# Routing logits and ranks of a mixture of experts: 32-column weights and moving tokens in place of 128-column weights, with a transpose behind

## Chip, cores and metric

The kernel runs on one core of one Trainium2 chip. The metric is the device time of an execution in microseconds. Three runs of the kernel before gave 1860.09, 1860.68 and 1863.35 us, median 1860.68.

## What is computed

The reference is a two-layer gated block over x, 16 batches of 256 tokens with 256 features. Each layer adds an attention part and a feed-forward part. Only the first feed-forward part, a router with 8 experts, is touched by the change:

```python
logits = x @ router_w.T                       # x: 4096 normed tokens x 256, router_w: 8 x 256
probs = softmax(logits, axis=-1)
topk_vals, topk_idx = top_k(probs, 2)
topk_w = topk_vals / (topk_vals.sum(-1, keepdims=True) + 1e-06)
expert_out = einsum('nh,eho->eno', x, expert_weights)
combined = take_along_axis(expert_out.transpose(1, 0, 2), topk_idx[:, :, None], axis=1)
out = ((combined.transpose(1, 0, 2) + remap_bias) * weights).sum(axis=0)
```

Around it stand a cross-attention with 16 heads ahead (333 keys a batch), a cross-attention over 77 context rows behind, and a chunked gated linear attention at the end. All is in float32.

## The kernel before

The program has four stages, one after the other, and a second, slow version of them (`fast` false) behind a branch that the profiled execution does not take.

The first stage, `stage0_fast` (L564), is the first attention. It works in units of a batch b and a group g of four heads, 64 units. The order on each engine is written out by hand: `dve`, `act`, `pool` and `pe` are `Pinned` (L42), which keeps every instruction in program order. A unit does, in this order: `scores(b, g)` (TensorE, then exponentials on ScalarE), `sums` on GpSimd, then `values` of the unit before (rows named o), and by g: `turn` and `project` at g = 1, `all_values(b + 1)` at g = 2, and always `heads` (rows named qk) of the unit ahead. `values` ends in two VectorE instructions, a reciprocal and a product (L742, L743). TensorE's o matmuls write four column tiles: head h goes to partitions 32h to 32h + 31 (L725, L739). `heads` leaves its keys to a VectorE copy (L690) and its queries to ScalarE (L689).

PSUM is handed out in pairs of banks, four of them in turn (L569 to L575): each new tile takes the pair used four tiles ago, once its reader is done.

The router's work for earlier batches is slipped between these steps by three tables (L761 to L767). `route.logits` of batch b - 1 stands behind `values` at g = 3 and `route.ranks` of batch b - 2 behind `values` at g = 2. Those of the last batches stand in the second stage, in its own table (L1201), beside the experts' matmuls.

- `logits` (L428): with the normed tokens turned to `xnT` (features on partitions), the tokens are the stationary operand, 128 tokens a time, and the router's 8 columns move. Four matmul calls a batch write tokens on partitions, 16 columns. ScalarE copies them to SBUF (`copied`, L436). `exps` and `choose` (L441, L450) find the two experts of every token.
- `ranks` (L507) counts, for each token and expert, the tokens ahead of it in the batch that go to the same expert: a triangle `before` and a square of ones are stationary, the choices `hs` move (16 columns each). ScalarE copies 32 columns. `place` (L514) turns the counts into rows.
- `scatter` writes each token's weighted copies to the experts' rows in DRAM by an indirect DMA from GpSimd.

`clear_rows` (L555) fills those rows with zeros ahead of it: 16 DMAs of 640 KB on SP's queue, from a tile of 128 x 256 zeros that is read repeatedly. It is called in the second unit (L810), and SP takes its instructions in order; the stores of the context's values (L662) and the load of them for batch 1 (L664) come behind it.

The second stage multiplies the experts' rows; the third and fourth are the second layer. In the fourth, a step in `stage3_fast` (L1858 to L1873) writes sums to four column tiles, with the rows `den`, and turns them back by a VectorE transpose, rows `dens`. It is in the kernel already and is not edited.

Of the kernel before, what the change touches and what calls it, by code (L numbers as in the profile page):

```python
# [10 lines left out]
F32 = mybir.dt.float32  # L11
I32 = mybir.dt.int32
AF = mybir.ActivationFunctionType
ALU = mybir.AluOpType
# [3 lines left out]
P = 128  # L18
B, S, D = 16, 256, 256
# [7 lines left out]
def bc(ap, shape, *axes):  # L27

    for a in axes:
        ap = ap.unsqueeze(a)  # L30
    return ap.to_broadcast(list(shape))
# [42 lines left out]
def layers(ctx: ExitStack, tc: tile.TileContext, t, out, check):  # L74
    nc = tc.nc
# [6 lines left out]
    def const(name, shape, dtype=F32):  # L82
        return cp.tile(list(shape), dtype, tag=name, name=name)
# [11 lines left out]
    def load_w(name, rows, cols, pool=cp):  # L95
        w = pool.tile([P, rows // P, cols], F32, tag=name, name=name)
        src = t[name].rearrange("(k p) f -> p k f", p=P)
        step = min(rows // P, max(1, (1 << 20) // (P * cols * 4)))
        for k in range(0, rows // P, step):
            nc.sync.dma_start(out=w[:, k:k + step, :], in_=src[:, k:k + step, :])  # L100
        return w
# [4 lines left out]
    ws1 = s1.enter_context(tc.tile_pool(name="s1w", bufs=1, side="right"))  # L106
# [34 lines left out]
    wo0 = load_w("wo0h" if fast else "wo0", 1024, D, w0)  # L141
    for b in range(2, B):
        load_x(b)
    rw1 = load_w("rw1", D, 8, ws1)
    ew1 = load_w("ew1", D, 2048, ws1)
    prio = const("prio", [P, 8])
    nc.sync.dma_start(out=prio, in_=t["prio"])
# [1 line left out]
    if fast:  # L149
        bv, own, pmask = (w12.tile(shape, F32, tag=n, name=n) for n, shape in (  # L150
            ("bv", [P, D]), ("own", [P, 2, 32]), ("pmask", [P, 2])))
        before, offs = (ws1.tile(shape, F32, tag=n, name=n) for n, shape in (
            ("before", [P, P]), ("offs", [P, 2, 2, 8])))

        gbo = const("gbo", [P, D])
        for n, x in (("bv", bv), ("bo", gbo), ("own", own), ("pmask", pmask), ("before", before),
                     ("offs", offs)):
            nc.sync.dma_start(out=x, in_=t[n])
    else:
        brow = w12.tile([1, 2, D], F32, tag="brow", name="brow")  # L160
        nc.sync.dma_start(out=brow, in_=t["brow"])
        bmask = w12.tile([P, 4], F32, tag="bmask", name="bmask")
        nc.sync.dma_start(out=bmask, in_=t["bmask"])
# [4 lines left out]
    ones = const("ones", [P, P])  # L168
# [6 lines left out]
    dve, act, pool, pe = (Pinned(tc, x) for x in (nc.vector, nc.scalar, nc.gpsimd, nc.tensor))  # L175
# [219 lines left out]
    class Route:  # L395
# [31 lines left out]

        def logits(self, b, bank):  # L428
            ps, xnT = bank("rt"), self.xnT.pop(b)
            for i in range(2):  # L430
                for k in range(2):
                    pe.matmul(ps[:, 8 * i:8 * i + 8], xnT[:, k, i * P:(i + 1) * P], rw1[:, k, :],
                              start=k == 0, stop=k == 1)
            self.copied(b, ps[:, :16])

        def copied(self, b, ps):  # L436
            n = ps.shape[1]
            self.ps[b] = ws1.tile([P, n], F32, tag=f"copied{n}", name="copied")
            act.copy(self.ps[b], ps)

        def exps(self, b):  # L441

            z = self.ps.pop(b)[:, :16].rearrange("p (i e) -> p i e", i=2)
            mx = st.tile([P, 2], F32, tag="rmx", name="rmx")
            dve.tensor_reduce(mx, z, AX.X, ALU.max)
            e = self.e[b] = st.tile([P, 2, 8], F32, tag="re", name="re")
            dve.tensor_tensor(e, z, bc(mx, [P, 2, 8], 2), ALU.subtract)
            act.activation(e, e, AF.Exp)
# [58 lines left out]
        def ranks(self, b, bank):  # L507
            hs, h1, h2 = self.hs[b]
            ps = bank("rank")
            pe.matmul(ps[:, :16], before, hs[:, 0].rearrange("p i e -> p (i e)"), start=True, stop=True)  # L510
            pe.matmul(ps[:, 16:32], ones, hs[:, 1].rearrange("p i e -> p (i e)"), start=True, stop=True)
            self.copied(b, ps[:, :32])

        def place(self, b):  # L514

            (_, h1, h2), ps, count = self.hs.pop(b), self.ps.pop(b), check["rows"][:, b // 8]
            base = st.tile([P, 2, 2, 8], F32, tag="base", name="base")
            at = st.tile([P, 2, 2, 2, 8], F32, tag="at", name="at")
            row = st.tile([P, 2, 2, 2], F32, tag="row", name="row")
            n = st.tile([P, 2, 8], F32, tag="nth", name="nth")  # L520
            dve.tensor_tensor(n, ps[:, :16].rearrange("p (i e) -> p i e", i=2), bc(count, [P, 2, 8], 1), ALU.add)
            dve.tensor_tensor(count, count, ps[:, 24:32], ALU.add)
            dve.tensor_tensor(n[:, 1, :], n[:, 1, :], ps[:, 16:24], ALU.add)
            dve.tensor_tensor(base[:, 0], n, offs[:, 0], ALU.add)

            dve.scalar_tensor_tensor(base[:, 1], n, ROWS - 1.0, offs[:, 1], ALU.min, ALU.add)
            for k, h in enumerate((h1, h2)):
                dve.tensor_tensor(at[:, :, :, k], base, bc(h, [P, 2, 2, 8], 1), ALU.mult)
            dve.tensor_reduce(row, at, AX.X, ALU.add)
            dve.tensor_copy(self.pos[:, b], row)  # L530
# [19 lines left out]
    def by_expert(rows, e):  # L550

        n = ALL_ROWS if rows in route.rows else ROWS
        return rows[e * n:e * n + ROWS].rearrange("(p n) d -> p n d", p=P)

    def clear_rows():  # L555
        zero = ws1.tile([P, D], F32, tag="zero", name="zero")
        nc.gpsimd.memset(zero, 0.0)
        n = ROWS // P
        for rows in route.rows:
            for e in range(8):  # L560
                nc.sync.dma_start(out=by_expert(rows, e),
                                  in_=bc(zero, [P, n, D], 1))

    def stage0_fast():  # L564
        with ExitStack() as sx:
# [339 lines left out]
    def stage1():  # L905
        with ExitStack() as sx:
# [4 lines left out]
            def bank(name):  # L911
                return pss.tile([P, 512], F32, tag="ps", name=name)

            def route(b):
                xn = w2.tile([P, 2, D], F32, tag="xn", name="xn")
                layernorm(xn, xs[b], P, 2)
                xnT = normed_T(w3_, bank, xn)
                ps = bank("rt")
                for i in range(2):
                    for k in range(2):  # L920
                        nc.tensor.matmul(ps[:, 8 * i:8 * i + 8], xnT[:, k, i * P:(i + 1) * P], rw1[:, k, :],
                                         start=k == 0, stop=k == 1)
                shape = [P, 2, 8]
                pr = softmax_last(st, "pr", ps[:, :16].rearrange("p (i e) -> p i e", i=2), shape)
                m1, h1 = first_max("a", pr, shape)
                p2 = st.tile(shape, F32, tag="p2", name="p2")
                nc.vector.scalar_tensor_tensor(p2, h1, -2.0, pr, ALU.mult, ALU.add)
                m2, h2 = first_max("b", p2, shape)
                f = st.tile([P, 2], F32, tag="f", name="f")
                nc.vector.scalar_tensor_tensor(f, m1, 1e-6, m2, ALU.add, ALU.add)  # L930
                nc.vector.reciprocal(f, f)
                nc.vector.tensor_scalar(f, f, gate[:, 1:2], None, ALU.mult)
                wt = st.tile(shape, F32, tag="wt", name="wt")
                nc.vector.tensor_tensor(wt, h1, h2, ALU.add)
                nc.vector.tensor_tensor(wt, wt, pr, ALU.mult)
                nc.vector.tensor_tensor(wt, wt, bc(f, shape, 2), ALU.mult)
                nc.vector.tensor_tensor(p2, wt, pr, ALU.mult)
                add = st.tile([P, 2], F32, tag="add", name="add")
                nc.vector.tensor_reduce(add, p2, AX.X, ALU.add)
                return xnT, wt, add  # L940
# [1199 lines left out]
def _arrays(i):  # L2140

    f = {k: np.asarray(v) for k, v in i.items()}
    z = np.zeros

    def cols(v):
# [15 lines left out]
    s, u, h = r[:, None], r[None, :], r[None, :64]  # L2161
# [16 lines left out]
        "x": f["x"], "ctx": f["ctx_1024"], "fside": f["fside_BxSxS2_0"], "mask": f["mask_BxSxS2_ik1"], "vec": vec,  # L2178
        "wkv0": f["L0_xattn_Wkv"], "wq0": f["L0_xattn_Wq"], "wo0": f["L0_xattn_Wo"],
        "wo0h": f["L0_xattn_Wo"].reshape(4, 4, 2, 32, D).transpose(0, 2, 1, 3, 4).reshape(1024, D),  # L2180
        "rw1": f["L0_ffn_router_w"].T, "ew1": f["L0_ffn_expert_weights"].transpose(1, 0, 2).reshape(D, 2048),
        "prio": np.broadcast_to(np.arange(8, 0, -1, dtype=np.float32), (P, 8)),
        "wq2": f["L1_xattn_wq_k"], "wk2": f["L1_xattn_wk_k"], "wv2": f["L1_xattn_wv_k"], "wo2": f["L1_xattn_wo_k"],
        "brow": np.stack([f["L1_xattn_wv_b"], f["L1_xattn_wo_b"]])[None], "bmask": bmask.astype(np.float32),
        "la": la, "lbk": lbk, "lbg": lbg, "we3": f["L1_ffn_We"],
        "wq3": f["L1_ffn_Wq"], "wk3": f["L1_ffn_Wk"], "wv3": f["L1_ffn_Wv"], "wo3": f["L1_ffn_Wo"],
        "before": (s < u) * np.float32(1),
        "offs": np.broadcast_to(np.float32([ALL_ROWS, ROWS]).reshape(2, 1, 1) * np.arange(8, dtype=np.float32), (P, 2, 2, 8)), "smask": smask, "halves": halves.astype(np.float32),
        "dmask": dmask.astype(np.float32), "amask": amask.astype(np.float32),
    }  # L2190
# [16 lines left out]
```

## Time and profile before

| what | before |
|---|---|
| median of three runs | 1860.68 us |
| profiled execution, its own time | 1860.41 us |
| its span, first to last instruction | 1858.6 us |
| mean granted TensorE clock | 0.998 |
| first stage, a batch in the middle (586.50 to 646.15) | 59.65 us |
| in that batch busy: DVE, ACT, POOL | 36.30, 24.58, 38.47 us |
| rt (logits), TensorE instructions, median of one | 128, 256 ns |
| rank with before, with ones, TensorE instructions | 32 and 32, 263 ns each |
| ScalarE copies of rt and rank, median of one | 172 and 185 ns |
| transpose of 128x256 from PSUM on VectorE (dens), median | 442 ns |
| clearing DMAs (rows<-zero), issued | 37.1 to 61.4 us |

The time of an execution is a little longer than its span; the difference, 1.8 us, lies outside the instructions. In a row of the profile, PE is a matmul and PEld the load of its stationary operand; "128\*32 128x256" means 128 rows and 32 columns of the array in use and 256 moving columns. One matmul call in float32 appears as two instructions of each kind. A matmul's duration runs from its start until its results are out, and the next one starts long before that: what a group of matmuls takes from TensorE is read from the start of the group to the start of the next, not from durations.

### The profile page before, as it was taken

The page shows a single profiled execution, that of the slowest core. Times are in us where ns is not written, and L with a number is a line of the kernel's source. Part 1 is how long each engine was busy: PE and PEld are TensorE (multiplying, and loading weights), DVE is VectorE, ACT ScalarE, POOL GpSimd, SP SyncE. Part 2 cuts the span into 40 slices and gives each one's busy share as a digit, 9 for nine tenths or more (in the row PEclk, how much of TensorE's full clock was granted, in tenths as well). Part 3 has the DMA queues.
Part 4 walks back from the last instruction along what each step waited for, and adds up shares of the span by engine and source line. Part 5 has one row for each costly group of instructions (what it writes and reads, how often), then busy time and mean ns, then how long its engine had stood idle before and what let it go on. Part 6 is the DMA issues. An engine that isn't in the chain of part 4 may idle for free.

```text
span 1858.6 us, 34765 instructions
## 1 busy us (share of the span) xinstructions
PE 1833.0 (99%) x13678; PEld 1270.8 (68%) x13678; DVE 1231.4 (66%) x2903; ACT 863.9 (46%) x1804; POOL 1016.0 (55%) x1001
## 2 busy tenths in 40 slices
PE   8999999999999999999999999999999999999997
PEld 5666666666766667666777766667777777777775
DVE  3345656556655656555465388878888888888874
ACT  4433344343443434434343487845544545454542
POOL 4654767567666576656634767314444444444443
PEclk9999999999999999999999999999999999999999
DMA  9500010000010000000068933100000000000000
GB/s 322 204 3 20 18 32 15 25 16 22 24 37 7 29 20 10 28 24 19 10 213 249 250 50 48 18 1 1 12 7 7 7 12 7 7 7 7 13 7 14
DMA packets 56902, 84.62 MB, mean 46 GB/s; under 512 B 10467, under 2 KB 44371, under 8 KB 56217
## 3 DMA queue, kind: packets, MB, share of 16 engines
q1 hardware_dynamic: 44441, 65.52, 10.7%
q0 software_dynamic: 12288, 16.79, 4.5%
q8 instruction: 110, 1.80, 0.4%
q14 instruction: 63, 0.52, 0.1%
HBM read 44.00 MB, written 38.29 MB: 44 GB/s over the span
## 4 chain that ended last, share of the span: by engine, by line
PE 94%; DVE 2%; ACT 1%; POOL 1%; issue 1%; DMA 0%; SPq 0%; POOLq 0%; DVEq 0%; ACTq 0%
PE o L50 14%; PE qk L50 13%; PE sc L50 11%; PE v L50 9%; PE proj L50 7%; PE kq L1635 7%; PE sc L1635 5%; PE gq L1635 3%; PE ex L50 3%; PE v L1635 3%; PE proj L1635 3%; PE o L1635 3%; PE gz L1635 2%; PE low L1635 1%; PE ms L1635 1%; PE q L50 1%
## 5 line engine op out<-in xcount | busy, mean ns | idle before, releaser
L50 POOL TENSOR_SCALAR rs<-mv 128x2 f32<-128x2 f32 (+2 forms) x85 | 16.2, 191 | 395.4 <-DVE mv L50 393.2
L50 DVE RECIPROCAL rd<-o 128x256 f32<-128x256 f32 x64 | 112.4, 1756 | 162.6 <-PE o L50 162.6
L50 ACT ACTIVATE e<-sc 128x1024 f32<-128x1024 f32 (+1 forms) x192 | 181.5, 1015 | 18.5 <-PE sc L50 18.5
L50 PE MATMUL sc<-qk 64*128 64x256 f32 (+1 forms) x1536 | 183.1, 384 | 0.5 <-DVE qk L50 0.5
L50 PE MATMUL o<-e,v 128*32 128x256 f32 (+1 forms) x3072 | 177.9, 379 | 0.0
L50 PEld LDWEIGHTS sc<-qk 64*128 64x128 f32 (+1 forms) x1536 | 132.1, 172 | 55.0 <-issue 26.8
L50 POOL TENSOR_TENSOR esum<-esum,es 128x512 f32<-128x512 f32 x128 | 163.2, 1275 | 10.0
L50 PE MATMUL qk<-kvT,wkv 128*128 128x333 f32 x512 | 164.3, 443 | 0.0
L50 POOL TENSOR_TENSOR es<-e 128x1024 f32<-128x1024 f32 x64 | 151.2, 2363 | 13.7 <-ACT e L50 10.6
L50 POOL TENSOR_TENSOR at<-at,at 128x768 f32<-128x768 f32 x63 | 114.0, 1809 | 74.5 <-DVE at L50 73.6
L50 ACT ACTIVATE qk<-qk 128x256 f32<-128x256 f32 x128 | 48.9, 382 | 227.1 <-PE qk L50 227.1
L50 POOL TENSOR_TENSOR es<-es,e 77x1024 f32<-77x1024 f32 x64 | 150.3, 2348 | 5.0
L50 PEld LDWEIGHTS o<-e,v 128*32 128x32 f32 (+1 forms) x3072 | 99.8, 110 | 66.4
L50 DVE COPY qk<-qk 128x333 f32<-128x333 f32 x128 | 64.6, 505 | 106.8 <-ACT qk L50 104.9
L50 PE MATMUL qk<-kvT,wq 128*128 128x256 f32 x512 | 134.4, 385 | 0.0
L50 POOL DMA_INDIRECT x<-rows_out,pos x64 | 100.9, 1577 | 34.7 <-issue 17.2
L50 PEld LDWEIGHTS qk<-kvT,wkv 128*128 128x128 f32 x512 | 97.2, 190 | 30.0
L50 PEld LDWEIGHTS qk<-kvT,wq 128*128 128x128 f32 x512 | 94.4, 189 | 33.7 <-issue 13.7
L50 PE MATMUL proj<-wo0h,oT 128*128 128x256 f32 x512 | 113.5, 380 | 0.0
L50 PE MATMUL v<-wkv,kvT 128*128 128x512 f32 x256 | 113.0, 594 | 0.0
L50 POOL TENSOR_TENSOR gw<-zs,eg 128x512 f32<-128x512 f32 x32 | 40.7, 1273 | 120.5 <-ACT eg L50 115.8
L50 PEld LDWEIGHTS proj<-wo0h,oT 128*128 128x128 f32 x512 | 96.0, 190 | 13.3 <-issue 0.8
(261 smaller groups left out, 4124.4 us busy)
## 6 DMA issues: line engine op xcount, KB each, us to landing
rows<-zero SPq DMA_DIRECT2D x16, 640.0 KB
xin<-rows SPq DMA_DIRECT2D x16, 640.0 KB
rows_out<-y SPq DMA_DIRECT2D x16, 384.0 KB
v<-vctx SPq DMA_DIRECT2D x15, 308.0 KB
x<-in_x_dram SPq DMA_DIRECT2D x16, 256.0 KB
rows_out<-y SPq DMA_DIRECT2D x16, 256.0 KB
out_dram<-x SPq DMA_DIRECT2D x15, 256.0 KB
wkv<-in_wkv_dram SPq DMA_DIRECT2D x2, 1024.0 KB
```

The costliest lines, as they stand in the source:

```text
L50: x = getattr(self.engine, name)(*a, **k)
L1635: tc.keep_in_program_order(nc.tensor.matmul(*a, **k))
```

## The change

In `logits` the operands change places. The router's weights, padded with zeros from 8 to 32 columns in DRAM, become the stationary operand, and the tokens move. Four column tiles q each take 64 tokens: 32 of each half of the batch. Tile q writes partitions 32q to 32q + 31, of which 8 carry logits, and 64 columns. For each of the two halves k of the features there are four calls. A VectorE transpose in 32x32 blocks (`turned`) brings tokens back on partitions, and takes the place of ScalarE's copy. `exps` reads the first 8 of 32 columns.

In `ranks` the choices `hs` (2 x 2 x 8 = 32 columns) become stationary and the triangle moves. `before` gets a fifth block of 32 columns that holds ones. Tile q moves block q and the block of ones, in one call. Again a transpose takes the place of the copy, and `place` reads the same numbers at other positions.

The tile of zeros shrinks from 256 to 128 columns, and each clearing DMA reads it twice as often for the same bytes.

```diff
-    rw1 = load_w("rw1", D, 8, ws1)
+    rw1 = load_w("rw1", D, 32, ws1)
...
-            ("before", [P, P]), ("offs", [P, 2, 2, 8])))
+            ("before", [P, 5, 32]), ("offs", [P, 2, 2, 8])))
...
         def logits(self, b, bank):
             ps, xnT = bank("rt"), self.xnT.pop(b)
-            for i in range(2):
-                for k in range(2):
-                    pe.matmul(ps[:, 8 * i:8 * i + 8], xnT[:, k, i * P:(i + 1) * P], rw1[:, k, :],
+            for k in range(2):
+                for q in range(4):
+                    pe.matmul(ps[32 * q:32 * q + 32, :64], rw1[:, k, :],
+                              xnT[:, k, :].rearrange("p (i q t) -> p i q t", i=2, q=4)[:, :, q, :],
                               start=k == 0, stop=k == 1)
-            self.copied(b, ps[:, :16])
-
-        def copied(self, b, ps):
-            n = ps.shape[1]
-            self.ps[b] = ws1.tile([P, n], F32, tag=f"copied{n}", name="copied")
-            act.copy(self.ps[b], ps)
+            self.turned(b, ps)
+
+        def turned(self, b, ps):
+
+            self.ps[b] = ws1.tile([P, 2, 32], F32, tag="turned", name="turned")
+            dve.transpose(self.ps[b].rearrange("p n e -> p (n e)"), ps[:, :64])
...
-            z = self.ps.pop(b)[:, :16].rearrange("p (i e) -> p i e", i=2)
+            z = self.ps.pop(b)[:, :, :8]
...
             ps = bank("rank")
-            pe.matmul(ps[:, :16], before, hs[:, 0].rearrange("p i e -> p (i e)"), start=True, stop=True)
-            pe.matmul(ps[:, 16:32], ones, hs[:, 1].rearrange("p i e -> p (i e)"), start=True, stop=True)
-            self.copied(b, ps[:, :32])
+            for q in range(4):
+                pe.matmul(ps[32 * q:32 * q + 32, :64], hs.rearrange("p w i e -> p (w i e)"),
+                          before[:, q:5:4 - q, :], start=True, stop=True)
+            self.turned(b, ps)
...
-        zero = ws1.tile([P, D], F32, tag="zero", name="zero")
+        zero = ws1.tile([P, P], F32, tag="zero", name="zero")
...
-                nc.sync.dma_start(out=by_expert(rows, e),
-                                  in_=bc(zero, [P, n, D], 1))
+                nc.sync.dma_start(out=by_expert(rows, e).rearrange("p n (x d) -> p (n x) d", d=P),
+                                  in_=bc(zero, [P, 2 * n, P], 1))
```

Left out are the slow version's read of the padded weights (it takes the first 8 columns), the new positions in `place`, and the padding of the two arrays on the host.

More of the change, by code (lines that the diff above doesn't have):

```diff
@@ L520, in place @@
             n = st.tile([P, 2, 8], F32, tag="nth", name="nth")
-            dve.tensor_tensor(n, ps[:, :16].rearrange("p (i e) -> p i e", i=2), bc(count, [P, 2, 8], 1), ALU.add)
-            dve.tensor_tensor(count, count, ps[:, 24:32], ALU.add)
-            dve.tensor_tensor(n[:, 1, :], n[:, 1, :], ps[:, 16:24], ALU.add)
+            dve.tensor_tensor(n, ps[:, 0, :16].rearrange("p (i e) -> p i e", i=2), bc(count, [P, 2, 8], 1), ALU.add)
+            dve.tensor_tensor(count, count, ps[:, 1, 24:32], ALU.add)
+            dve.tensor_tensor(n[:, 1, :], n[:, 1, :], ps[:, 1, 16:24], ALU.add)
             dve.tensor_tensor(base[:, 0], n, offs[:, 0], ALU.add)
@@ L920, in route @@
                     for k in range(2):
-                        nc.tensor.matmul(ps[:, 8 * i:8 * i + 8], xnT[:, k, i * P:(i + 1) * P], rw1[:, k, :],
+                        nc.tensor.matmul(ps[:, 8 * i:8 * i + 8], xnT[:, k, i * P:(i + 1) * P], rw1[:, k, :8],
                                          start=k == 0, stop=k == 1)
@@ L2180, in _arrays @@
         "wo0h": f["L0_xattn_Wo"].reshape(4, 4, 2, 32, D).transpose(0, 2, 1, 3, 4).reshape(1024, D),
-        "rw1": f["L0_ffn_router_w"].T, "ew1": f["L0_ffn_expert_weights"].transpose(1, 0, 2).reshape(D, 2048),
+        "rw1": np.concatenate([f["L0_ffn_router_w"].T, z((D, 24), np.float32)], axis=1), "ew1": f["L0_ffn_expert_weights"].transpose(1, 0, 2).reshape(D, 2048),
         "prio": np.broadcast_to(np.arange(8, 0, -1, dtype=np.float32), (P, 8)),
@@ L2186, in _arrays @@
         "wq3": f["L1_ffn_Wq"], "wk3": f["L1_ffn_Wk"], "wv3": f["L1_ffn_Wv"], "wo3": f["L1_ffn_Wo"],
-        "before": (s < u) * np.float32(1),
+        "before": np.concatenate([(s < u) * np.float32(1), np.ones((P, 32), np.float32)], axis=1).reshape(P, 5, 32),
         "offs": np.broadcast_to(np.float32([ALL_ROWS, ROWS]).reshape(2, 1, 1) * np.arange(8, dtype=np.float32), (P, 2, 2, 8)), "smask": smask, "halves": halves.astype(np.float32),
```

## Prediction

> **What bounds the kernel now.** I read the page's first part, then the busy time by stretches, then the PE timeline of one batch of the first stage, and last the other engines in the same batch.
>
> ```profile
> PE 1833.0 (99%) x13678; PEld 1270.8 (68%) x13678; DVE 1231.4 (66%) x2903; ACT 863.9 (46%) x1804; POOL 1016.0 (55%) x1001
> ```
>
> By stretches (PE, PEld, DVE, ACT, POOL busy us and counts, clock, DMA share, GB/s), the first stage's repeating part:
>
> ```profile
> 98.00:933.00 835.00, 834.89 (x6554) 557.47 (x6552) 485.29 (x1193) 341.88 (x676) 533.79 (x478) 1.00 0.06 20
> ```
>
> In these 835 us PE is idle for 0.11 us; DVE is busy 58%, ACT 41%, POOL 64%. So a nanosecond taken from PE's stream is a nanosecond of the kernel, and work added to DVE or taken from ACT counts only if it makes PE wait. The page's clock is full throughout. What PE spends on routing is read by comparing the same passage with and without it (start, length, instructions):
>
> ```profile
> 589.97 2.78 PE L50 MATMUL o<-e,v 128*32 128x256 f32 x48
> 592.68 1.06 PE L50 MATMUL rt<-rw,rxnT 128*128 128x8 f32 x8
> 593.59 1.11 PE L50 MATMUL qk<-kvT,wq 128*128 128x256 f32 x4
> 594.54 1.28 PE L50 MATMUL qk<-kvT,wkv 128*128 128x333 f32 x4
> ...
> 600.99 2.78 PE L50 MATMUL o<-e,v 128*32 128x256 f32 x48
> 603.70 1.13 PE L50 MATMUL qk<-kvT,wq 128*128 128x256 f32 x4
> 604.67 1.28 PE L50 MATMUL qk<-kvT,wkv 128*128 128x333 f32 x4
> ...
> 628.75 2.78 PE L50 MATMUL o<-e,v 128*32 128x256 f32 x48
> 631.46 0.40 PE L50 MATMUL rank<-hs,before 128*128 128x16 f32 x2
> 631.70 0.38 PE L50 MATMUL rank<-hs,ones 128*128 128x16 f32 x2
> 631.93 3.68 PE L50 MATMUL v<-wkv,ctxT 128*128 128x512 f32 x8
> 635.44 7.03 PE L50 MATMUL v<-wkv,kvT 128*128 128x512 f32 x16
> ```
>
> From the start of o to the second qk group: 594.54 - 589.97 = 4.57 us with rt, 604.67 - 600.99 = 3.68 us without. **rt costs 0.89 us a batch.** For rank the partner is batch 0, which has none yet:
>
> ```profile
> 48.43 2.78 PE L50 MATMUL o<-e,v 128*32 128x256 f32 x48
> 51.14 3.70 PE L50 MATMUL v<-wkv,ctxT 128*128 128x512 f32 x8
> 54.68 7.03 PE L50 MATMUL v<-wkv,kvT 128*128 128x512 f32 x16
> ```
>
> 635.44 - 628.75 = 6.69 us against 54.68 - 48.43 = 6.25 us: **rank costs 0.44 us a batch.** Both rows are weight loads rather than products: 8 instructions in 0.89 us are 112 ns each, for 8 moving columns.
>
> **What the skill says.** "TensorE: Matmul & The Clock Gate", LDWEIGHTS: the load takes the stationary tile's columns divided by 1.2 GHz, 107 ns for 128 and 27 ns for 32. The 112 ns above agree. "TensorEngine Tiling (Array Packing)", Key Properties: tiles load and multiply independently, and a change of tiling mode drains the engine. The trace agrees with both: 12 rounds of four o matmuls at 216 ns would be 2.59 us, and o takes 2.71 us to the next row, so leaving the mode costs 0.12 us; and the four tiles of a round start 7 ns apart in the instruction records. "TensorE: Matmul & The Clock Gate", "Wait — 56ns, not 53.3ns?": starts are never closer than about 25 ns. The 7 ns contradict that for different column tiles, but only in bursts; I keep it as a bound.
>
> **PE, the part that pays.** A logical f32 matmul is two instructions here (8 in rt for 4 calls). New logits: 2 k x 4 tiles x 2 = 16 instructions, in four rounds of four; new ranks: 4 x 2 = 8, two rounds. Each has a load of 32 columns and 64 moving columns. Price of a round: 256 columns take 217 ns (qk) and 512 take 429 ns (v, 6.87 us for 16), so 0.83 ns a column and 4 ns beside it; 64 columns stream in 57 ns. The next 32-column loads lie under that, if they overlap as o's do (about 27 ns by the skill; o's first, uncovered round is 24 ns longer). The trace shows no 64-column round on four tiles. Bounds: 57 ns from below (a cheaper round is excluded, the columns have to stream), and from above 25 ns a start, 100 ns a round. I take 60. The changes of mode stay: o, rt and rank are now all 128*32, so the drain that lay before rt lies behind it, with the same exposed first load of qk as where there is no rt.
> - rt: 4 x 0.06 = 0.24, saves 0.65 us; 15 batches have it in the first stage (L767, offset -1): 9.8 us.
> - rank: 2 x 0.06 = 0.12, saves 0.32 us; 14 batches (offset -2): 4.5 us.
> - In the second stage (ranks 14, logits 15, ranks 15) the neighbours are 128*128, so the new form pays two changes of mode, about 0.25 us with loads. Logits: 0.81 before (960.33 to 961.14), about 0.5 after, 0.3 gained. Ranks: 0.37 before, about 0.37 after. 0.2 in sum.
>
> Sum 14.5 us.
>
> **ACT and DVE.** ACT loses copies of 172 and 185 ns a batch; it only waited for qk next, so nothing comes of it. DVE gains two transposes of 128x64 from PSUM. Nearest row: dens in the last stage, 128x256 in 442 ns; copies of 128x512 and 128x256 take 692 and 419 ns, 1.07 ns an element, so 442 - 192 x 1.07 = 237 ns. Between 150 (the fixed part of small DVE operations) and 440 ns. Where it stands in DVE's order:
>
> ```profile
> 592.82 1.76 DVE L50 RECIPROCAL rd<-o 128x256 f32<-128x256 f32 x1 [2.02 <-PE o L50]
> 594.61 0.69 DVE L50 TENSOR_TENSOR oT<-o,rd 128x512 f32<-128x512 f32 x1
> 596.34 0.51 DVE L50 COPY qk<-qk 128x333 f32<-128x333 f32 x1 [1.04 <-ACT qk L50]
> ```
>
> The transpose waits for rt, which has ended (about 593.0) before DVE is through with oT at 595.30, so that wait is empty. Queued behind it is the copy of qk, for which PE's scores wait. DVE ends at 595.54; ACT, which the copy waits for, ended at 596.30 and will at about 595.65. Cover 0.1 us left; if it were gone, the second copy has 1.42 us of idle time before it, so nothing reaches PE. For ranks the stream transposes of rxnT stand behind, then the copy of vc after 1.02 us of idle time. The rt bank is freed at 595.54 instead of 593.94 by ACT; it is needed again four pairs later, by the second score group near 598. All hidden: 0, at most 1 us in sum.
>
> **DMA and queues.** rw1 and before: a few more bytes at the start, nothing waits. clear_rows: 16 transfers of 640 KB, now in 512 B packets, 20480 instead of 10240. It saturates the DMA engines from 37 us to about 65. "DMA: Bandwidth & Descriptors", "Why small descriptors are slow", puts a fixed cost on each packet; in the packet records of this trace 512 B take 27 ns and 1024 B 46 ns. So 20480 x 27 / 16 = 34.6 us instead of 29.4: 5.1 us later. Behind it on SP are the vctx stores (63.07), the load of v for batch 1 (issued 70.13) and loads of c. PE first needs that v at 89.10 (o of batch 1). Issued near 75.3, and with at most the 5.1 us that the stores took to land, it is there by 80.4: hidden with 8.7 us to spare. SP's own issue is 0.62 us where it isn't held back (the first of the 16), so twice the packets fit beside the transfers.
>
> **Sum.** The profiled execution took 1860.41 us (span 1858.6 and 1.8 around it), 0.3 below the median of the three, 1860.68. 1860.4 - 14.5 = 1845.9; against the median 1846.2. I say 1846.0.
>
> **Rivals.**
> - Issue-bound rounds, part of the likeliest case's range: 100 ns a round. rt 0.40, rank 0.20; 15 x 0.49 + 14 x 0.24 = 10.7 us, 1849.7.
> - No gain: PE feeds small pairs no faster than o shows on average, 2.71 us / 48 = 56 ns each. 16 x 56 = 0.90 and 8 x 56 = 0.45, just what stands there now: 1860. Against: four starts within 21 ns. For: o is the densest stream in the trace, and no longer burst is seen. 6%.
> - Slower: the loads of the four column tiles don't overlap when the matmul is too short to cover them, and each pair keeps the 112 ns of rt's present row. 16 x 112 = 1.79 and 8 x 112 = 0.90 us: 15 x 0.90 + 14 x 0.46 = 20 us more, 1880. It decides at 56 ns a pair, the break-even. Against: a load of 32 columns is a quarter of one of 128. 4%.
> - v of batch 1 comes late: if 512 B packets took 46 ns too, clearing would last 29 us longer, v would land at 101 to 104 instead of before 89, and PE stand 12 to 15 us once: 1858 to 1861. Against: the 27 ns. 5%.
>
> **How the numbers follow.** Likeliest (57 to 100 ns a round, all else hidden): 85%; it alone is faster by over 0.2% (3.7 us, about what a measurement of this kernel can tell from no change), and the third rival's lower end by a little. Faster 0.86, same 0.09, slower 0.05. Range: 1843.0 (57 ns a round and 2 us between runs) to 1852.0 (100 ns, and as much again).
>
> **What would show it.** Right: from o's start to the second qk group 3.9 us where rt stands, 6.37 with rank; rt starts in rounds of four; transposes of 235 ns on DVE without a wait before them; PE still without idle time; the first o of batch 1 not delayed. Wrong: rt as long as now (issue), or longer (loads), or an idle PE after 85 us named by the v load.

## The result and the profile after

| what | before | after |
|---|---|---|
| median of the runs (lowest to highest) | 1860.76 us (1860.09 to 1863.35, 4 runs) | 1849.39 us (1846.71 to 1850.70, 4 runs) |
| ratio, with its 95% interval | | 0.9932 [0.9918, 0.9945] |
| profiled execution, its own time / span | 1860.41 / 1858.6 us | 1848.33 / 1846.5 us |
| PE in its first stage, from its first unit to its last (batch 15, g = 3) | | 12.4 us shorter |
| the whole span | | 12.1 us shorter |

The kernel became 0.7% faster, 11.4 us between the medians; 14.5 us were forecast. The page's first line and the busy time of the first stage's repeating part (columns as before: PE, PEld, DVE, ACT, POOL with counts, clock, DMA share, GB/s):

```profile
PE 1818.5 (98%) x13870; PEld 1258.0 (68%) x13870; DVE 1253.5 (68%) x2935; ACT 858.4 (46%) x1772; POOL 1017.4 (55%) x1001
```

```profile
98.00:933.00 835.00, 832.58 (x6839) 555.75 (x6838) 516.62 (x1249) 341.32 (x662) 542.62 (x482) 1.00 0.07 23
```

PE has 192 instructions more and is busy 14.5 us less. But in a stretch of 835 us in which it was idle for 0.11 us it is now idle for 2.42 us (the stretch now ends where the second stage begins). TensorE's order of the batch whose rows were shown of before, with the passages of rt and rank:

```profile
583.62 2.78 PE L50 MATMUL o<-e,v 128*32 128x256 f32 x48
586.22 0.41 PE L50 MATMUL rt<-rxnT,rw 128*32 128x64 f32 x16
586.55 1.13 PE L50 MATMUL qk<-kvT,wq 128*128 128x256 f32 x4
587.52 1.28 PE L50 MATMUL qk<-kvT,wkv 128*128 128x333 f32 x4
...
603.93 0.64 PE L50 MATMUL o<-es,ones 128*32 128x256 f32 x8 [0.23 <-POOL es L50]
...
622.03 2.78 PE L50 MATMUL o<-e,v 128*32 128x256 f32 x48
624.63 0.30 PE L50 MATMUL rank<-before,hs 128*32 128x64 f32 x8
624.85 3.70 PE L50 MATMUL v<-wkv,ctxT 128*128 128x512 f32 x8
628.39 7.03 PE L50 MATMUL v<-wkv,kvT 128*128 128x512 f32 x16
```

The passage with rt takes 587.52 - 583.62 = 3.90 us (4.57 before), the one with rank 628.39 - 622.03 = 6.36 us (6.69 before). Against the same passages with neither (3.68 and 6.25 us), rt costs 0.22 us and rank 0.11: six rounds of four at 55 ns each. And the row at 603.93 carries a bracket that no o row had before: PE waits for es, the sums of exponentials that GpSimd adds up (`sums`). Of PE's waits in the first stage just two are new. Their lines over the whole span (us in total, times, longest):

```profile
PE o L50 <- POOL es L50: 2.1, 8, 0.4
PE proj L50 <- DVE oT L50: 2.1, 4, 0.9
```

The first line was not there at all; the second was 1.7, 3, 0.9, all of it behind the first stage. Where the first comes from stands in GpSimd's order ahead of that o. Before, with the first row of the chain on top:

```profile
590.28 0.19 POOL L50 TENSOR_SCALAR rs<-mv 128x2 f32<-128x2 f32 x1 [7.05 <-DVE mv L50]
...
604.30 1.08 POOL L50 DMA_INDIRECT rows<-xw,pos  x1 [0.18 <-issue]
605.40 2.38 POOL L50 TENSOR_TENSOR es<-e 128x1024 f32<-128x1024 f32 x1
607.86 2.35 POOL L50 TENSOR_TENSOR es<-es,e 77x1024 f32<-77x1024 f32 x1
```

and PE's row of the same unit in the kernel before:

```profile
610.66 0.64 PE L50 MATMUL o<-es,ones 128*32 128x256 f32 x8
```

After:

```profile
583.93 0.19 POOL L50 TENSOR_SCALAR rs<-mv 128x2 f32<-128x2 f32 x1 [6.70 <-DVE mv L50]
...
597.97 1.08 POOL L50 DMA_INDIRECT rows<-xw,pos  x1 [0.17 <-issue]
599.08 2.37 POOL L50 TENSOR_TENSOR es<-e 128x1024 f32<-128x1024 f32 x1
601.53 2.35 POOL L50 TENSOR_TENSOR es<-es,e 77x1024 f32<-77x1024 f32 x1
```

Before, es ended at 607.86 + 2.35 = 610.21, 0.45 us ahead of its reader. After, it ends at 603.88, and PE, which is 0.67 us faster in the passage, is ready for it at 603.70 and starts at 603.93, 0.05 us behind its end. Ahead of es GpSimd works without a gap of more than half a microsecond from 583.93 on: eight small operations for norms, a scatter, es and esum of one unit, four more norm operations, a second scatter. **That chain takes 610.21 - 590.28 = 19.93 us before and 603.88 - 583.93 = 19.95 after; only its reader came closer.** The chain's start was not delayed by the new transposes: it lies 0.31 us behind the start of the o row ahead of rt in both kernels (589.97 and 583.62). GpSimd is that full in the seven batches in which norms of a context fall between. There each logits step of 0.67 us gives 0.2 to 0.3 back, and one more unit, near 193 us in the kernel before, gives back 0.5.

VectorE, in the passage at 586 us:

```profile
588.26 0.69 DVE L50 TENSOR_TENSOR oT<-o,rd 128x512 f32<-128x512 f32 x1
588.87 0.24 DVE L50 STREAM_TRANSPOSE turned<-rt 128x64 f32<-128x64 f32 x1
589.32 0.51 DVE L50 COPY qk<-qk 128x333 f32<-128x333 f32 x1 [0.21 <-ACT qk L50]
```

The transpose waits for nothing and takes 240 ns. The copy behind it has 0.21 us of idle time left of 1.04: still hidden. And SP's queue:

```profile
38.84 36.11 SPq L563 DMA_DIRECT2D rows<-zero  x16
75.04 5.30 SPq L664 DMA_DIRECT2D vctx<-vc  x3
82.16 0.28 SPq L666 DMA_DIRECT2D v<-vctx  x1
```

The load of v for batch 1 is issued at 82.16, not near 75.3 (70.13 before). Yet the first o of batch 1 starts at 89.17, against 89.10 before.

Added up by the starts of the same PE groups in both traces: 14 ranks steps of -0.33 us, 14 logits steps of -0.67, and one of -0.88 at the end of the stage, where rt stands between two o groups and both changes of mode fall away: -14.9 us. The waits for es give 2.5 back, which leaves -12.4. The last batch gives back 0.5, the second and third stage 1.7 net, the fourth gains 0.3, and the part from TensorE's last step to the end is 1.6 us shorter: -12.1.

### The profile page after: what moved, and what is told of

It is laid out like the page before. It is cut to its first block, busy times and chain, and to the rows that moved or that the text cites. A ratio compares the mean times of both kernels' runs of the same rounds, so it can differ in the third digit from the quotient of the medians.

```text
span 1846.5 us, 35163 instructions
## 1 busy us (share of the span) xinstructions
PE 1818.5 (98%) x13870; PEld 1258.0 (68%) x13870; DVE 1253.5 (68%) x2935; ACT 858.4 (46%) x1772; POOL 1017.4 (55%) x1001
## 4 chain that ended last, share of the span: by engine, by line
PE 85%; POOL 7%; DVE 4%; ACT 2%; issue 1%; DMA 1%; SPq 0%; POOLq 0%; ACTq 0%; DVEq 0%
PE o L50 11%; PE qk L50 11%; PE v L50 9%; PE sc L50 8%; PE proj L50 7%; PE kq L1637 7%; PE sc L1637 6%; POOL es L50 4%; PE gq L1637 3%; PE v L1637 3%; PE proj L1637 3%; PE o L1637 3%; PE ex L50 3%; PE gz L1637 2%; POOL rs L50 2%; PE low L1637 2%
## 5 line engine op out<-in xcount | busy, mean ns | idle before, releaser
L50 POOL TENSOR_TENSOR es<-e 128x1024 f32<-128x1024 f32 x64 | 151.3, 2364 | 12.1 <-ACT e L50 9.0
```

Of the source, the lines that this page charges most:

```text
L50: x = getattr(self.engine, name)(*a, **k)
```

## Experiments

Each was timed beside the kernel before on the same chip; there the kernel before gave medians of 1860.69 to 1861.39 us. Unless a row says otherwise an edit is made in the changed kernel, and "first stage" is the shift of TensorE's starts over it against the kernel before.

### Each half alone

Theory: the waits for es belong to the logits, since only their saving (0.67) exceeds the slack of 0.45 us. Rival: they come from the transposes on VectorE or from any shortening. First the logits alone, with the ranks as before (and their copy on ScalarE):

```diff
-            for q in range(4):
-                pe.matmul(ps[32 * q:32 * q + 32, :64], hs.rearrange("p w i e -> p (w i e)"),
-                          before[:, q:5:4 - q, :], start=True, stop=True)
-            self.turned(b, ps)
+            pe.matmul(ps[:, :16], before.rearrange("p q t -> p (q t)")[:, :P], hs[:, 0].rearrange("p i e -> p (i e)"), start=True, stop=True)
+            pe.matmul(ps[:, 16:32], ones, hs[:, 1].rearrange("p i e -> p (i e)"), start=True, stop=True)
+            self.copied(b, ps[:, :32])
```

Left out are `copied`, which comes back, and the old positions in `place`.

> Only the logits in the new form; the ranks, their ScalarE copy and their place in the second stage as before (the triangle's four blocks serve as the 128-column weights). My theory: each logits step takes 0.67 us off PE (0.89 to 0.22), 15 times, and in the seven batches in which GpSimd also has a context norm in that passage it gives about 0.3 us back at the first o of the next batch, where PE then waits for es. So 10.1 + 0.2 (the step beside two o groups) - 2.1 = 8.2 us at the end of the first stage, about 1852 to 1853 in all. Rival, that the waits for es come from both transposes on VectorE together: fewer waits, about 10 us, 1850.

1855.00 us, ratio 0.9966 [0.9958, 0.9974]. First stage -7.8 us; each logits step is -0.67, and the line of waits for es reads 1.9 us in 8. The first stage is near the 8.2 us expected; the time lies 2 us above the expected 1852 to 1853. In the profiled execution PE's clock was at half for 10.2 us near the border of the third and fourth stage, which cost 4.9 us there.

Then the ranks alone, with the logits as before:

```diff
-            for k in range(2):
-                for q in range(4):
-                    pe.matmul(ps[32 * q:32 * q + 32, :64], rw1[:, k, :],
-                              xnT[:, k, :].rearrange("p (i q t) -> p i q t", i=2, q=4)[:, :, q, :],
+            for i in range(2):
+                for k in range(2):
+                    pe.matmul(ps[:, 8 * i:8 * i + 8], xnT[:, k, i * P:(i + 1) * P], rw1[:, k, :8],
...
-            self.turned(b, ps)
+            self.copied(b, ps[:, :16])
```

Left out are `copied` and the old slice in `exps`.

> Only the ranks in the new form; the logits with tokens as weights and a ScalarE copy as before. My theory: 14 times 0.33 us, 4.7 us at the end of the first stage, and no wait of PE for es, since the passage with the tight GpSimd chain (from the logits group to the next batch's first o) keeps its length: about 1856. Rival, waits from the transposes on VectorE: PE waits for es here too, about 1857 to 1858.

1857.40 us, ratio 0.9981 [0.9974, 0.9988]. First stage -4.6 us, 14 times 0.33, and from 98 to 935 us no wait of PE at all. The time is 1.4 us above the expected 1856. The shifts of the two halves add up to the change's 12.4 us. Both halves pay, and the waits go with the logits. VectorE's transposes of the ranks cause none.

### GpSimd's scatter behind the sums

If the es chain is what takes the 2.5 us back, the scatter (1.1 us on GpSimd), which stands in front of es, can be moved behind `sums`. No work is left out.

```diff
-            behind_scores = {0: [(normed_all, 1), (route.scatter, -3, 1)],
+            behind_scores = {0: [(normed_all, 1)],
...
+            behind_sums = {0: [(route.scatter, -3, 1)]}
...
                 now = sums(*now)
+                run(behind_sums, b, g)
...
             run(behind_scores, B, 0)
+            run(behind_sums, B, 0)
```

> The changed kernel with one of GpSimd's four scatters a batch (the one in the first unit of a batch) moved behind that unit's exponent sums instead of ahead of them. My theory: GpSimd's chain up to es is 1.1 us shorter there, PE's eight waits for es (2.1 us in the profile of the change) are gone, every logits step keeps its 0.67 us, and the first stage ends about 2 us earlier: 1847.3 against the change's 1849.4. Rival, es is late because VectorE's statistics start GpSimd late or because something else comes last a moment later (exponentials, VectorE's copy): the waits move to another name and the time stays within 0.5 us of the change.

1845.51 us (1844.39 to 1846.49), ratio 0.9916 [0.9896, 0.9936]. GpSimd in the same unit:

```profile
598.91 2.34 POOL L50 TENSOR_TENSOR es<-es,e 77x1024 f32<-77x1024 f32 x1
601.33 2.67 POOL L50 TENSOR_TENSOR esum<-esum,es 128x512 f32<-128x512 f32 x2
604.17 1.08 POOL L50 DMA_INDIRECT rows<-xw,pos  x1 [0.18 <-issue]
```

and PE's wait, over the whole span:

```profile
PE o L50 <- POOL es L50: 0.4, 1, 0.4
```

The DMA_INDIRECT now stands behind esum; seven of the eight waits are gone; the one near 193 us, in another unit, is left. First stage -14.5 us. To see whether the gain holds in time, the changed kernel and this one were run together once more, unedited otherwise:

> The change itself once more, beside the next kernel on the same chip: 11 to 13 us under the kernel before, PE's eight waits for es as in the first profile (about 2 us), the mask loads of the second stage early or late by chance (0.4 us gained or up to 0.9 us lost there).

> The change with the late scatter once more: 2 us under the change on the same chip, if the first comparison was no luck; its profile shows no more than one wait for es. Rival, the gain of 3.9 us seen between different runs was mostly a difference in the granted clock: the two are within 1 us of each other.

The changed kernel gave 1850.18 us, ratio 0.9943 [0.9929, 0.9957], the late scatter 1847.03, ratio 0.9933 [0.9919, 0.9946]. The 3 us between the medians are one more than expected. In the traces the first stage ends 2.1 us earlier, and the waits for es are 2.0 us in 8 against 0.4 in 1. The ratios' intervals overlap this time, and 1.6 us of the difference between these two profiles is chance: in the profile of the changed kernel alone, PE's granted clock fell to half for 3.41 us at 1210 us (0.83 as a mean from 1206 to 1216). The executions with the highest granted clock, 0.999, took 1847.44 us for the change and 1844.94 and 1845.66 with the late scatter. So the 2.1 us are shown in the traces, and the times agree with them without fixing their size.

### The second stage as before

Theory: the +0.30 us by which the second stage is longer in the change comes from a mask that is loaded there and arrives late, not from the new form between matmuls of 128 columns. The last batches take the old form, whose calls and copies are those of the two edits above:

```diff
+        def logits(self, b, bank):
+            (self.logits_old if b == B - 1 else self.logits_new)(b, bank)
+
+        def ranks(self, b, bank):
+            (self.ranks_old if b >= B - 2 else self.ranks_new)(b, bank)
```

> The changed kernel, but in the second stage (ranks of 14, logits and ranks of 15) the old form: tokens and triangle as weights, copies on ScalarE. My theory from the traces: the new form gained 0.5 us there at first, and 0.7 us were lost a little later to a mask load that came late; if that load follows the DMA chain and not the routing step, the time is the same within 1 us as the change. Rival, the transposes in a stretch where VectorE is busy throughout cost what was lost: up to 0.7 us faster than the change.

1847.54 us, ratio 0.9929 [0.9909, 0.9949], not told apart from the change. The second stage shifts by +0.53 with the old form, but at other places: PE waits 0.25 us longer for ScalarE's xT, and 0.24 us for VectorE's hs ahead of the second ranks. So the run shows that the old form is no better; it does not show where the change's own loss comes from. For that the traces speak: after a gain of 0.36 us in the passage of the logits, the change loses 0.73 us in the step behind VectorE's wait for the mask.

```profile
982.46 0.74 DVE L50 TENSOR_REDUCE mm<-mk 77x1 f32<-77x256 int32 x2 [0.89 <-DMA mk<-in_maskT_dram]
```

That was the row before; after:

```profile
968.77 0.74 DVE L50 TENSOR_REDUCE mm<-mk 77x1 f32<-77x256 int32 x2 [2.28 <-DMA mk<-in_maskT_dram]
```

In the other versions that route this stage as the change does, the loss grows with the longest such wait: none at 1.64 us (late scatter), 0.5 at 2.05 (the change once more), 1.4 at 2.90 (the clearing in 1 KB packets, below). That agrees with the theory, but no run changed the mask's arrival alone.

### The clearing DMAs

The size of the packets was a rival (a late v). First the packets of 1 KB again, with the zeros in a buffer that stands unused at that time:

```diff
-        zero = ws1.tile([P, P], F32, tag="zero", name="zero")
+        zero = ws1.tile([P, 2, 2, D], F32, tag="xw0", name="xw")[:, 0, 0, :]
...
-                nc.sync.dma_start(out=by_expert(rows, e).rearrange("p n (x d) -> p (n x) d", d=P),
-                                  in_=bc(zero, [P, 2 * n, P], 1))
+                nc.sync.dma_start(out=by_expert(rows, e),
+                                  in_=bc(zero, [P, n, D], 1))
```

> The changed kernel with the clearing in 1 KB pieces as before (the zeros lie in a buffer that is used later for weighted rows, since a tile of 256 columns of its own no longer fits). My theory: clearing ends about 12 us earlier, the load of v for batch 1 is issued near 70 instead of 82 us, and PE doesn't notice: first stage the same to 0.1 us, total the same as the change. Rival, the longer clearing costs something in the change: faster by the 0.5 to 1 us that it would have to be.

1848.94 us, ratio 0.9936 [0.9917, 0.9954]; first stage -12.7, as the change. The smaller packets cost nothing. The load of v for batch 1 was issued at 75.23 us, not near the expected 70, so of the 12 us by which it is later in the change the packets' size accounts for about 7. Then packets of 256 B, to see how near the edge was:

```diff
-        zero = ws1.tile([P, P], F32, tag="zero", name="zero")
+        zero = ws1.tile([P, P // 2], F32, tag="zero", name="zero")
...
-                nc.sync.dma_start(out=by_expert(rows, e).rearrange("p n (x d) -> p (n x) d", d=P),
-                                  in_=bc(zero, [P, 2 * n, P], 1))
+                nc.sync.dma_start(out=by_expert(rows, e).rearrange("p n (x d) -> p (n x) d", d=P // 2),
+                                  in_=bc(zero, [P, 4 * n, P // 2], 1))
```

> The changed kernel with the clearing in 256 B pieces: 40960 packets. 256 B took 18 ns in the trace of before, so 46 us at least, and with the tenth by which the 512 B packets exceeded their price, about 51 us against the change's 40. The load of v for batch 1 is then issued near 93 us and lands near 96; PE needs it at 89.2 and should stand for about 7 us at the first o of batch 1: about 1856. If clearing has other cover than I think, no stall and 1849.

1858.18 us, ratio 0.9982 [0.9974, 0.9989]. PE at the first o of batch 1:

```profile
89.19 1.05 PE L50 MATMUL o<-e,v 128*32 128x256 f32 x16
96.68 3.64 PE L50 MATMUL o<-e,v 77*32 77x256 f32 x32 [6.44 <-DMA v<-vctx]
100.25 1.12 PE L50 MATMUL tr<-ident,xn 128*128 128x128 f32 x4
```

The load was issued at 92.85 and PE stood for 6.44 us. The step is 9.6 us, more than the wait: the 8 rounds behind it take 100.25 - 96.68 = 3.57 us, 446 ns a round where o has 216. The granted clock was at half from 92.63 to 102.87 us. That cost, about 3 us, was not in the expected 1856. The rival's mechanism is real. The change stops one step short of it.

### Four times the logits

The rivals on the price of a pair (54 to 56 ns: no gain; 112 ns: slower) speak of long bursts, and a round of 0.06 us is too short to exclude that the next row hides something. So the logits were computed four times over:

```diff
-            for k in range(2):
+            for k in [0, 1] * 4:
```

> The changed kernel with the logits' matmuls run four times over (the first three passes are overwritten; the result is the same): 16 rounds of four instead of 4. My theory: a round of four tiles with 64 columns takes 56 ns however long the burst is; 12 more rounds are 0.67 us a batch, 15 times, 10 us, less what the waits for es swallow (2.1 us): about 1857. Rival, PE can feed such rounds only from its filled queue, and slows to 25 ns a start (100 ns a round) or to 54 ns a pair (216 ns a round) in a longer burst: 1.2 or 2.6 us a batch, 1865 or 1886.

1860.82 us, ratio 1.0003 [0.9992, 1.0014]. In the trace, the first row from an earlier batch:

```profile
245.97 0.64 PE L50 MATMUL rt<-rxnT,rw 128*32 128x64 f32 x27 [0.30 <-issue]
...
589.16 2.78 PE L50 MATMUL o<-e,v 128*32 128x256 f32 x48
591.76 1.08 PE L50 MATMUL rt<-rxnT,rw 128*32 128x64 f32 x64
...
593.74 1.28 PE L50 MATMUL qk<-kvT,wkv 128*128 128x333 f32 x4
```

593.74 - 589.16 = 4.58 us against 3.90 for 16 instructions: 48 more cost 0.68 us, 56 ns a round, 14 ns a pair. The price holds over 64 pairs where the burst is not broken, and both rivals are excluded. In nine of the fifteen batches the logits step is now what it was before the change, and in the last it is 0.3 us shorter. The waits for es are gone, which fits: their reader is as late as it was. In the other five the burst is broken once, as in the row at 245.97, which starts after 0.30 us in which PE waited for nothing that the profile shows ("issue"); these five steps are 0.59 to 1.07 us longer, 3.5 us in sum. With that, and 2.3 us that the second and third stage lose, goes the gain of the ranks; the expected 1857 was missed by 4 us. Why the instructions stall there is open. In the changed kernel, with a quarter of the pairs, no wait of this kind is seen.

### Both edits

The late scatter and the old form in the second stage together:

> The late scatter and the old form in the second stage together. My theory: about 2 us under the change, 1847 to 1847.5.

1847.74 us, ratio 0.9927 [0.9913, 0.9940]; first stage -14.5 as with the late scatter alone, and no gain beside it: the clock fell to half near 1209 and 1229 us of its profile, for 3.4 and 6.8 us, which cost 4.8 us, and the second stage lost 0.9. The best version is the change with the late scatter: faster than the kernel before in both sets of runs, and ahead of the change by 2.1 us in the first stage of the trace.

## Why the prediction was right, and where it was not

- **PE's price: right.** 0.06 us a round were taken; 0.056 came. rt 0.89 to 0.22 (0.24 forecast), rank 0.44 to 0.11 (0.12). Gross -14.9 us for the first stage against 14.3, the difference being the last logits step, where two o groups are neighbours and 0.88 falls away instead of 0.65, and 0.01 or 0.02 us in each of the others. Costing the old form by comparing the passage with and without it, not by durations, gave the right number.
- **The bound from the Trainium skill, 25 ns a start: did not bind.** "TensorE: Matmul & The Clock Gate", "Wait — 56ns, not 53.3ns?", has starts never below about 25 ns. With four column tiles the starts lie 14 ns apart on average over 64 pairs. An estimate from the same page's LDWEIGHTS section puts four loads of 32 columns, one after the other, at 4 x 27 = 107 ns; a round takes 56. So the loads of different column tiles do run together; in the records the four of a round start 5 to 8 ns apart and last 107 to 111 ns each.
- **"All hidden": the step that failed.** It covered ACT and DVE, with at most 1 us. GpSimd was read only as "POOL 64%" and its chain was not costed. The slack of es, 0.45 us, stood in the trace of before. The step that should have been taken: min(0.67, 0.45) in the seven batches where the chain is full. That gives 7 x 0.22 = 1.5 us back, and 1.9 with the 0.05 us between es and its reader; the rest of the 2.5 us measured is the unit near 193 us. The 2.5 us are shown by the waits, by each half alone and, all but 0.4, by the late scatter. They are the largest part of the 3.4 us between forecast and median.
- **VectorE: right for the passages that were costed** (237 ns forecast, 240 measured, 0.21 us of cover left). In the last batch, which was not costed, proj waits 0.34 us for oT where it did not before, and 0.5 us is lost: two o groups start 4 us apart there, and the transpose stands on VectorE between their products. The late scatter and the old form in the second stage both leave it; with the logits four times over, where the passage is longer, it is gone. It was not tried by itself.
- **Clearing: right in the end, wrong in the margin.** 5.1 us later and 8.7 us spare were forecast. The load was issued 12 us later, about 7 of them by the packets' size. With 256 B PE went on 3.8 us after the load was issued; by that v landed near 86 us in the change (an estimate), some 4 us before the matmuls that read these rows, which in the run with 256 B would have started at 90.24. The packets took 29.8 ns in the mean, not 27, which makes 38 us, and the rate was lower at first (233 GB/s from 45 to 48 us, then about 285). So the rival of the late v, put at 5%, was nearer than it looked; at 256 B it happens.
- **The second stage:** 0.2 us forecast. The passage of the logits did gain 0.36, but against the kernel before the stage moves between -0.4 and +0.9 us from one version to the next. With the new form this goes with the arrival of the mask, which VectorE awaits; both versions with the old form lose without a long wait for it.
- **Not explained:** 1.0 to 1.8 us gained behind TensorE's last step in every version, against the one profile of the kernel before. In the third stage two profiles of the changed kernel differ by 0.9 us; together with the halved clock this is the noise in which a single profile stands.

The forecast's sum with the measured steps, the es waits and the last batch in it is 14.9 - 2.5 - 0.5 = 11.9 us, 1848.5 for the profiled execution, which took 1848.33. The good agreement is partly luck, since the second and third stage and the end cancel.

## What to carry to other kernels

On an engine without idle time, price an edit by the distance between the starts of the neighbours, with and without the edited group; durations in a pipeline mislead. Then, for each engine that feeds the saturated one, find in the same passage how long before its reader the last producer ends: the gain of an edit is capped there by that slack, whatever the engine's busy share is. If the slack is short, look for work in front of the producer that nobody waits for at once, and put it behind.

## What was not expected of the hardware

- Rounds of four column tiles with 64 moving columns in float32 keep 56 ns over 16 rounds, 14 ns for a load and a matmul; but in five bursts of fifteen of that length the engine stood still once for 0.30 to 0.40 us, with no wait that the profile shows.
- A pause of PE cost more than itself. After 6.44 us of waiting, the rounds of o took 446 ns instead of 216. The Trainium skill, "TensorE: Matmul & The Clock Gate", "What's actually happening", has the clock at half after an idle window of about 3.4 us. The run agrees that the pause halves the clock; here it fell 2.4 us into the pause (from 90.24 to 92.63 us), sooner than after a whole idle window, and came back 6.2 us after its end. That does not tell why the clock also fell, in five of the later profiles, for 3.41 us or three times that between the third and the fourth stage, where PE had only short waits.
- Stores of zeros from SBUF to DRAM, with all DMA engines busy: 385 GB/s in 1 KB packets in the kernel before, but 345 in the changed kernel, where the zeros lay in another buffer; 285 in 512 B and about 215 in 256 B. The 10.5 MB took 29 us before and 40 in the change. Why the two rates with 1 KB differ is open.
